# Grouped steps at the two ends of a stretch: block maxima from the copies, sums by a product with ones, separate PSUM banks for pairs and single items

## The chip, the cores and the metric

The kernel runs on one core of one Trainium2 chip. The metric is the device time of one execution in microseconds (us); the median of 3 runs of the kernel before is 3428.8 us (3427.73 to 3429.0). Engines are named as in the profile: PE multiplies matrices (its weight loads, PEld, run beside it), DVE is the vector engine, ACT the scalar engine, POOL the GpSimd engine, SP issues DMAs.

## The reference

Four cross-attention layers follow each other on x, of shape (4 batches, 512 positions, 256 channels), with a context of shape (4, 1024, 512), all in float32. Layers 0, 2 and 3 have 16 heads of 64, two columns of keys that a mask suppresses, a bias and a residual ("masked" layers). Layer 1 has an RMS norm ahead, 16 query heads of 16, and 4 heads of keys and values that four query heads share each ("grouped" layer).

```python
# layers 0, 2, 3
q, k, v = hidden @ Wq, context @ Wk, context @ Wv          # 16 heads of 64
logits = einsum('bhqd,bhkd->bhqk', q, k) * 64 ** -0.5 + col_bias
out = softmax(logits) @ v                                   # per head
x = out @ Wo + bo + hidden
# layer 1
xn = rmsnorm(x) * norm_w                                    # 16 heads of 16, 4 heads of k and v
x = x + (softmax(xn @ wq @ (context @ wk).T / 4) @ (context @ wv)) @ wo
```

## The kernel before, in words

**Units and steps.** A layer of a batch is cut into 8 units. A masked unit is two heads (64 rows each), a grouped unit two heads (of 16 rows, padded to 32). A unit's softmax stands with its 1024 keys in 8 blocks of 128 partitions and its two heads' 512 queries side by side, so one block is 128x1024 and fills two of the eight PSUM banks. The program has 96 steps (two strings, `MASKED_TURNS` and `GROUPED_TURNS`, say which unit comes when); each step has one masked unit `g`, and 32 of them, in four stretches of 8, have a grouped unit `lam` beside it. The batches are interleaved, so the grouped layer of one batch runs beside a masked layer of another. PE is given its instructions in the order of the program, and each engine works through its own in order.

**What a step does.** In order: `scores(g)` (L859): 8 blocks of logits, two matmuls each (L869; the first block also takes the mask by two small products, L875), each block copied by ACT from PSUM into the store `st` (L879). `attend(g1)` (L902): the products of the exponentials of the step before with the values, 16 matmuls of 64 columns. Then a list `fill` of PE work: output projections (L1108), the next queries (L766), keys (L552) or values (L605) of later units (in steps without grouped units by L665, with seven products for eight), among them `attend(lam)`. If the next step has a grouped unit, `coming`, its logits are made in this step as four **pairs** of blocks (`logits_pair`, L842 and the copy L848), which a list `pairs` sets between the entries of `fill` by a clock that adds up written estimates, 12.0 + 2.5 i.

**Maximum and exponentials.** The largest logit of each query is taken off. DVE spreads the maximum over all partitions (`max_quarters` L946 to L953, `max_everywhere` L966), then subtracts: DVE for masked units (L974), POOL for grouped ones (L972). ACT takes the exponentials (L980). POOL adds up the 8 blocks of a masked unit (`running_sum`, L1019); the sum over the partitions of that, and its reciprocal, come one step later. A grouped unit gets its sums from a column of ones in the values.

**Two ways, by a flag.** `tabled[0]` says for each step which way it goes; it is set where the step has a grouped unit and the next one has one too (`lam and coming`), 28 of the 96 steps.

- Flag off: block 0 stays in its two banks, DVE maximises the other 7 copies into it (L886 for scores, L857 for pairs: read PSUM and `st`, write PSUM) and reduces it (L926). Sums: `normalise` (L1066) late in the step: DVE alone, 10 instructions (L926, L1051 to L1062) and the scaling L1088. PSUM banks are taken from all eight, the longest free first.
- Flag on: each block's banks are given back after the copy, DVE reduces each copy to a column of a small table (`block_max`, L926 `tops<-st`) and the table at the end (L942). Sums: `sums_beside` (L1070), in the same step's `fill`: PE multiplies the running sum by ones (L1074, two matmuls of 64 columns, 4 records in the trace), DVE transposes, inverts and transposes back (L805 to L807), then L1088. Pairs of banks are taken from 0 to 3 (0 to 5 for scores), single banks from 4 to 7 (class `Place`, L103).

So a stretch of 8 grouped units has 7 steps of the second way, and at its ends two steps of the first: an **opening** step, with `coming` but no `lam` (they start at 378.22, 798.60, 1218.27 and 2426.59 us), and a **closing** step, with `lam` but no `coming` (719.63, 1139.30, 1558.77 and 2767.64 us). In an opening step the coming unit is the first of its batch; its queries (L781) and values (L743) are made at the head of `fill`. A bank is free for PE once its last reader is through: in these steps that is the copy of a block, the last subtraction (the two banks of the spread maximum, `mb_place`), the residual addition L1136 or L1140 (those of an output projection), the scaling L1088 (the bank `po` of `attend`) or `max_quarters`.

Of the kernel before, what the change touches and what calls it, by code (L numbers as in the profile page):

```python
# [20 lines left out]
NT = T // P  # L21
# [59 lines left out]
def kernel(ctx: ExitStack, tc: tile.TileContext, a: dict, out: bass.AP):  # L81
# [9 lines left out]
    def t_(shape, tag, name, bufs=1, dtype=FP):  # L91
        return sb.tile(shape, dtype, tag=tag, name=name, bufs=bufs)
# [8 lines left out]
    tabled = [False]  # L101
# [27 lines left out]
    def st_slot(n):  # L129
        return st_all[:, n // (NT + 1), n % (NT + 1), :]  # L130
# [6 lines left out]
    def give_set(g):  # L137
        sets_free.append(g.set)
# [660 lines left out]
    def reciprocal_rows(out_, in_, room):  # L799


        turned = room[:, 0:S]
        short = t_([P, S // 32, 1], "short", f"short{len(turns)}")
        turns.append(0)
        nc.vector.transpose(turned, in_)  # L805
        nc.vector.reciprocal(short, turned.rearrange("p (c r) -> p c r", r=32)[:, :, 0:1])
        nc.vector.transpose(  # L807
            out_.rearrange("p (c r) -> p c r", r=32), short.to_broadcast([P, S // 32, 32])
        )
# [3 lines left out]
    def norm_square(b):  # L813
        gq[b, "xn"] = t_([P, KC, S], "xn", f"xn{b}")
        nc.scalar.activation(gq[b, "xn"], xs[1, b], AF.Square)

    def rms_norm(b, room):
        x, xn, nw = xs[1, b], gq[b, "xn"], columns["L1_xattn_norm_w"]
        w = Place(1)
        m = w.ap  # L820
        for k in range(KC):
            nc.tensor.matmul(m, lhsT=ones, rhs=xn[:, k, :], start=(k == 0), stop=(k == KC - 1))

        def evacuate():
            inv = t_([P, S], "stage", f"inv{b}")
            nc.scalar.activation(inv, m, AF.Sqrt, bias=eps, scale=1.0 / C)
            w.back()
            reciprocal_rows(inv, inv, room)
            for k in range(KC):
                nc.vector.scalar_tensor_tensor(  # L830
                    xn[:, k, :], x[:, k, :], nw[:, k : k + 1], inv, ALU.mult, ALU.mult
                )

        return evacuate
# [53 lines left out]
    def place_out(g, width=1):  # L888
        g.place = Place(width)
        g.po, g.psum = g.place.ap[:, 0:S], g.place.ap[:, S:]  # L890

    def attend(g, blocks=range(NT)):
        for t in blocks:
            for j in range(2):
                rows = g.rows[j]
                if not g.masked:
                    rows = slice(64 * g.h + 32 * j, 64 * g.h + 32 * (j + 1))
                at, first, last = rows, 0, NT - 1
                if not g.masked:
                    at = slice(64 * (t % 2) + 32 * j, 64 * (t % 2) + 32 * (j + 1))  # L900
                    first, last = t % 2, NT - 2 + t % 2
                nc.tensor.matmul(  # L902
                    g.po[at, :], lhsT=g.v[:, t, rows], rhs=g.st[t][:, j * S : (j + 1) * S],
                    start=(t == first), stop=(t == last),
                )

    def keep_even(g):


        if g.h == 0:  # L910
            gq[g.b, "o"] = t_([P, S], "o1", f"o1_{g.name}")
        nc.scalar.copy(gq[g.b, "o"][64 * g.h : 64 * (g.h + 1), :], g.po[0:64, :])

    def keep_odd(g):
        half = gq[g.b, "o"][64 * g.h : 64 * (g.h + 1), :]
        nc.vector.tensor_tensor(half, half, g.po[64:128, :], ALU.add)
        if g.h == 0:
            g.place.back()
# [102 lines left out]
    def turn_grouped(g):  # L1021
        normalise_grouped(g, g.place.ap)
        g.place.back()
# [46 lines left out]
    def sums_beside(g):  # L1070
        w = Place(1, among=range(8))
        m = w.ap
        for j in range(2):
            nc.tensor.matmul(  # L1074
                m[g.rows[j], :], lhsT=ones[:, 0:64], rhs=g.acc[:, j * S : (j + 1) * S],
                start=True, stop=True,
            )

        def turned():
            g.ot = t_([P, S], "ot", f"ot_{g.name}", bufs=3)  # L1080
            reciprocal_rows(g.ot, m, g.ot)
            w.back()
            scale_out(g)

        return turned

    def scale_out(g):
        nc.vector.tensor_tensor(g.ot, g.po, g.ot, ALU.mult)  # L1088
        g.place.back()
# [99 lines left out]
    def at(n):  # L1189
        return steps[n] if 0 <= n < len(steps) else (None, None)  # L1190
# [8 lines left out]
    def head(g):  # L1199
        return steps[step_of[1, g.b, 0]][1]  # L1200
# [26 lines left out]
    g0, g1 = masked[0:2]  # L1227
# [24 lines left out]
    def keys(*of):  # L1252
        return [
            (1.7 if each.masked else 3.4, lambda h=h, part=part, each=each: k_part(each, h, part))
            for h in range(2 if of[0].masked else 1) for each in of for part in range(2)
        ]
# [27 lines left out]
    for n in range(len(steps) + 2):  # L1284
        g, lam = at(n)
        follows, coming = at(n + 1)
        tabled[0] = bool(lam and coming)
        soon = at(n + 2)[1]
        g1, attended = attended, g
        ending = n >= len(steps) - 2  # L1290
# [60 lines left out]
        late = []  # L1351
        pairs = []
# [5 lines left out]
        def behind_exponentials():  # L1358
            pass_events(99.0)
            while late:  # L1360
                late.pop(0)()
# [17 lines left out]
        by_ones = tabled[0]  # L1379
# [32 lines left out]
                    events.append((2.0 * t - 7.5, lam, lambda t=t: exponentials(lam, t)))  # L1412
            events.sort(key=lambda e: e[0])
        if coming:
            pairs += [(12.0 + 2.5 * i, i) for i in range(NT // 2)]

# [2 lines left out]
        def behind(add):  # L1421
            if g is not masked[-1]:
                return add
            late.append(add)

        fill, of_grouped = (
            [
                (1.8 * len(each), lambda each=each: behind(project_out(*each)))
                for each in outs if each[0].masked == m
            ]  # L1430
            for m in (True, False)
        )
# [4 lines left out]
        if fast_k:  # L1437
# [3 lines left out]
            fill = of_keys[:2] + fill + of_keys[2:4] + of_queries + of_keys[4:]  # L1441
        elif fast_v:
            of_values = fast_values(g)
            if fresh:
                of_values[1:4] = of_values[3:4] + of_values[1:3]
                fill = of_values[:2] + fill + of_grouped + of_values[2:4] + of_queries + of_values[4:]
                of_grouped = []
            else:
                fill = of_values[:2] + fill + of_queries + of_values[2:]
# [7 lines left out]
        if lam:  # L1457

            def attend_grouped():
                while any(of is lam for _, of, _ in events):  # L1460
                    events.pop(0)[2]()
                lam.v = head(lam).v
                place_out(lam)
                attend(lam)
                give_set(lam)
                late.append(lambda: keep_odd(lam))
                if lam.h == 1:
                    late.append(lambda: turn_grouped(lam))
                return lambda: keep_even(lam)

            total, where = 0.0, 0
            while where < len(fill) and total < (8.0 if by_ones and of_values else 9.5):
                total += fill[where][0]
                where += 1
            fill.insert(where, (3.6, attend_grouped))
            if by_ones:
                fill.insert(where, (1.0, lambda: late.insert(0, sums_beside(g1))))
        if soon and soon.first:

            def square():  # L1480
                behind_exponentials()
                norm_square(soon.b)

            of_keys = keys(soon)
            fill += of_keys[:1] + [(0.0, square)] + of_keys[1:]
            room = st_slot((NT + 1) * ctx_whole[soon.b][0] + NT)
            fill.append((1.7, lambda: rms_norm(soon.b, room)))
# [19 lines left out]
        for us, w in fill:  # L1507
            while pairs and pairs[0][0] <= now:
                pair(pairs.pop(0)[1])
                now += 1.0  # L1510
                pairs = [(max(at, now + 1.6), i) for at, i in pairs]
# [42 lines left out]
```

## Time and profile before

| | us |
|---|---|
| median of 3 runs | 3428.8 (3427.73 to 3429.0) |
| the profiled execution's own time | 3429.2 |
| its span, first to last instruction | 3427.4 (granted clock 0.999) |
| the four opening steps | 45.46, 45.17, 45.17, 45.41 |
| the four closing steps | 38.64, 38.64, 38.64, 38.65 |
| steps with the flag on, keys in `fill` (L552) | 43.46 to 45.48 |
| busy: PE, DVE, POOL, ACT | 3402.1, 2971.5, 2592.5, 2346.9 |

A step is measured from the start of its first L869 to that of the next step's. A line of the timeline gives the start, the time from the first to the end of the last of a row of equal instructions, the engine, line and shape, how many, and in brackets the idle time of the engine ahead of them with what ended it. Ends of matmuls are modelled, so the time that a row of matmuls takes is read here from its start to the start of the next row.

### The profile page before, as it was taken

To read this page: it belongs to the slowest core of one execution; us is meant where nothing else is said; L and a number is where in the kernel's file an instruction comes from. 1 tells how busy PE (TensorE), PEld (TensorE's weight loads), DVE (VectorE), ACT (ScalarE), POOL (GpSimd) and SP (SyncE) were. 2 spreads that over 40 slices of the span, in tenths; PEclk is the share of its full clock that TensorE was granted. 3 is DMA by queue.
4 is the path that set the end of the run, shared out by engine and by line. 5 is a ranking of instruction groups with operands and counts; after the bars stand their busy time and mean duration, and the time that the engine had idled before them with its cause. 6 is when DMAs were issued, how large, how long until landed. Compare 5 with 4: busy or idle time off the path is not lost.

```text
span 3427.4 us, 42731 instructions
## 1 busy us (share of the span) xinstructions
PE 3402.1 (99%) x15488; PEld 1652.1 (48%) x15488; DVE 2971.5 (87%) x3915; ACT 2346.9 (68%) x2729; POOL 2592.5 (76%) x1337
## 2 busy tenths in 40 slices
PE   9999999999999999999999999999999999999999
PEld 5555444444444444444455554554444445454554
DVE  7888889988889889998888888888888988889887
ACT  5666688776777767776656666666677866666665
POOL 4888488875888668888678768677588888769675
PEclk9999999999999999999999999999999999999999
DMA  3232111011100121011001111011101101011100
GB/s 105 67 114 86 57 36 51 30 48 37 54 27 30 48 62 30 27 30 45 28 28 53 34 36 43 28 53 56 37 30 51 36 21 53 28 40 56 35 30 10
DMA packets 147734, 151.70 MB, mean 44 GB/s; under 512 B 23608, under 2 KB 125496, under 8 KB 147012
## 3 DMA queue, kind: packets, MB, share of 16 engines
q1 hardware_dynamic: 144958, 140.58, 13.2%
q0 software_dynamic: 2560, 8.39, 0.9%
q8 instruction: 123, 2.02, 0.2%
q14 instruction: 87, 0.71, 0.1%
q10 hardware_dynamic: 6, 0.00, 0.0%
HBM read 132.15 MB, written 15.73 MB: 43 GB/s over the span
## 4 chain that ended last, share of the span: by engine, by line
PE 91%; DVE 7%; ACT 1%; issue 1%; DMA 0%; DVEq 0%; POOL 0%; ACTq 0%
PE ps L902 21%; PE ps L665 19%; PE ps L869 18%; PE ps L605 8%; PE ps L552 8%; PE ps L842 5%; PE ps L766 5%; PE ps L1108 5%; DVE ps L886 2%; DVE st L974 2%; PE ps L1074 1%; PE ps L567 1%; PE ps L875 1%; DVE ps L926 0%; PE ps L416 0%
## 5 line engine op out<-in xcount | busy, mean ns | idle before, releaser
L1019 POOL TENSOR_TENSOR st<-st 128x1024 f32<-128x1024 f32 x668 | 1581.5, 2367 | 566.3 <-ACT st L980 521.5
L980 ACT ACTIVATE st<-st 128x1024 f32<-128x1024 f32 x1024 | 1038.3, 1059 | 225.0 <-POOL st L972 109.7
L974 DVE TENSOR_TENSOR st<-st,ps 128x1024 f32<-128x1024 f32 x768 | 883.9, 1213 | 3.3
L902 PE MATMUL ps<-st,v 128*64 128x512 f32 (+1 forms) x4064 | 789.8, 595 | 0.0
L886 DVE TENSOR_TENSOR ps<-ps,st 128x1024 f32<-128x1024 f32 x476 | 586.7, 1233 | 210.9 <-ACT st L879 167.8
L972 POOL TENSOR_TENSOR st<-st 128x1024 f32<-128x1024 f32 x256 | 598.0, 2378 | 225.8 <-DVE st L966 185.4
L879 ACT COPY st<-ps 128x1024 f32<-128x1024 f32 x768 | 713.6, 1049 | 63.7 <-PE ps L875 58.2
L869 PE MATMUL ps<-qt,kt 64*128 64x512 f32 x3008 | 689.2, 596 | 4.0 <-DVE every L953 4.0
L926 DVE TRANSPOSE_TENSOR_REDUCE tops<-st 128x32 f32<-128x1024 f32 x448 | 517.6, 1212 | 43.6 <-ACT st L848 41.9
L902 PEld LDWEIGHTS ps<-st,v 128*64 128x64 f32 (+1 forms) x4064 | 239.9, 130 | 534.9 <-issue 447.5
L869 PEld LDWEIGHTS ps<-qt,kt 64*128 64x128 f32 x3008 | 280.9, 186 | 351.0 <-ACT st L879 143.8
L605 PE MATMUL ps<-wv,ctx 128*128 128x256 f32 x1344 | 313.7, 386 | 1.1 <-issue 1.1
L665 PE MATMUL ps<-st 128*128 128x128 f32 (+1 forms) x1620 | 308.6, 339 | 3.3 <-ACT ps L688 3.3
L552 PE MATMUL ps<-ctx,wk 128*128 128x512 f32 x672 | 310.4, 603 | 0.2 <-ACT ctx L428 0.2
L848 ACT COPY st<-ps 128x1024 f32<-128x1024 f32 x256 | 246.9, 1017 | 86.5 <-PE ps L842 85.8
L605 PEld LDWEIGHTS ps<-wv,ctx 128*128 128x128 f32 x1344 | 250.9, 191 | 93.1 <-issue 56.3
L665 PEld LDWEIGHTS ps<-st 128*128 128x128 f32 x1620 | 214.3, 192 | 95.5 <-issue 86.9
L680 ACT COPY st<-ps 128x512 f32<-128x512 f32 x45 | 26.4, 586 | 339.3 <-PE ps L665 339.3
L552 PEld LDWEIGHTS ps<-ctx,wk 128*128 128x128 f32 x672 | 122.0, 189 | 179.7 <-issue 163.4
L766 PE MATMUL ps<-x,wq 128*128 128x512 f32 x376 | 180.4, 602 | 1.1 <-ACT x L391 1.1
L842 PE MATMUL ps<-qt,kt 32*128 32x512 f32 x1024 | 171.5, 640 | 6.3 <-DVE ot L1088 5.2
L1108 PE MATMUL ps<-ot,wo 128*128 128x512 f32 x380 | 173.2, 598 | 0.0
(201 smaller groups left out, 3001.8 us busy)
## 6 DMA issues: line engine op xcount, KB each, us to landing
wv<-in_L_xattn_Wv_dram SPq DMA_DIRECT2D x48, 512.0 KB
ctx<-kept SPq DMA_DIRECT2D x24, 1024.0 KB
wk<-in_L_xattn_Wk_dram SPq DMA_DIRECT2D x47, 512.0 KB
wo<-in_L_xattn_Wo_dram SPq DMA_DIRECT2D x96, 128.0 KB
wq<-in_L_xattn_Wq_dram SPq DMA_DIRECT2D x94, 128.0 KB
st<-kept SPq DMA_DIRECT2D x4, 2048.0 KB
qt<-q SPq DMA_DIRECT2D x64, 128.0 KB
kept<-st SPq DMA_DIRECT2D x12, 512.0 KB
```

The costliest lines, as they stand in the source:

```text
L552: nc.tensor.matmul(m, lhsT=g.w["k"][:, k, :], rhs=ctx_half[g.b, n][:, k, :], start=(k == 0), stop=(k == KT - 1),)
L605: nc.tensor.matmul(m[:, half * 2 * P : (half + 1) * 2 * P], lhsT=ctx_half[g.b, t // 4][:, k, t % 4 * P : (t % 4 + 1) * P], rhs=g.w["v2"][: ...
L665: nc.tensor.matmul(m if is_keys else m[:, q], lhsT=right[:, k, :] if is_keys else left_[:, k, q], rhs=left_[:, k, :] if is_keys else right ...
L869: nc.tensor.matmul(m[:, j * S : (j + 1) * S], lhsT=g.kt[g.rows[j], keys], rhs=g.qt[g.rows[j], :], start=True, stop=t > 0,)
L879: nc.scalar.copy(g.st[t], m)
L886: nc.vector.tensor_tensor(top, top, g.st[t], ALU.max)
L902: nc.tensor.matmul(g.po[at, :], lhsT=g.v[:, t, rows], rhs=g.st[t][:, j * S : (j + 1) * S], start=(t == first), stop=(t == last),)
L926: nc.vector.tensor_reduce(out_, of.rearrange("p (b x) -> p b x", x=32), AX.X, op, apply_transpose=True)
L972: nc.gpsimd.tensor_tensor(g.st[t], g.st[t], g.mb, ALU.subtract)
L974: nc.vector.tensor_tensor(g.st[t], g.st[t], g.mb, ALU.subtract)
L980: nc.scalar.activation(st, st, AF.Exp)
L1019: nc.gpsimd.tensor_tensor(g.acc, g.st[0] if t == 1 else g.acc, g.st[t], ALU.add)
```

## The change

The flag is set for `lam or coming`, so the opening and closing steps go the second way as well: 36 steps in place of 28. The matmuls of `sums_beside` get a place in the `fill` of an opening step, and the clock of its pairs starts 1.0 later, which is what that entry adds to it. In a closing step the existing lines insert them ahead of `attend(lam)`. The choice of banks in `Place` and the branches in `scores`, `logits_pair` and `max_quarters` follow the flag and are not edited.

```diff
-        tabled[0] = bool(lam and coming)
+        tabled[0] = bool(lam or coming)
...
-            pairs += [(12.0 + 2.5 * i, i) for i in range(NT // 2)]
+            pairs += [((13.0 if coming.first else 12.0) + 2.5 * i, i) for i in range(NT // 2)]
...
             if by_ones:
                 fill.insert(where, (1.0, lambda: late.insert(0, sums_beside(g1))))
+        elif by_ones:
+            fill.insert(2, (1.0, lambda: late.insert(0, sums_beside(g1))))
```

In its order of instructions the changed program has on PE 16 matmuls L1074 more, two in each of the eight steps, and no other change of order; in an opening step they stand between L766 and the first L552, in a closing step between the third L552 group and the grouped L902. ACT and POOL have the same instructions in the same order. On DVE an opening step loses 7 L886, 7 L857, 2 L926 that read PSUM and the 10 instructions of L926 and L1051 to L1062, and gets 16 L926 that read the copies, 2 L942 and L805 to L807; a closing step the same without L857's half.

## The prediction

> **What bounds the kernel now.** First the page's busy times, then the waits of PE, then the timeline of PE in an opening and a closing step, last the same rows in a step that has the flag on already.
>
> ```profile
> PE 3402.1 (99%) x15488; PEld 1652.1 (48%) x15488; DVE 2971.5 (87%) x3915; ACT 2346.9 (68%) x2729; POOL 2592.5 (76%) x1337
> ```
>
> ```profile
> PE ps L842 <- DVE ot L1088: 5.2, 4, 1.3
> PE ps L869 <- DVE every L953: 4.0, 4, 1.2
> ```
>
> PE is busy 99% of the span, and its idle time is some 25 us. Two rows of waits are the largest, and each occurs four times: once in each opening step (a pair waits for L1088) and once in each closing step (a block of scores waits for L953).
>
> [...] Equal matmuls start at a fixed distance: 12 L552 of 128x512 take 5.24 us to the next row, 0.43 us each, in every step, and L902 x32 takes 7.02 us in all. A row that takes longer than its sisters has a wait in it. By that measure PE streams nearly everywhere, and what is to be gained is found row by row.
>
> An opening step, around its pairs:
>
> ```profile
> 820.94 1.88 PE L766 MATMUL ps<-x,wq 128*128 128x512 f32 x4
> 822.65 3.60 PE L552 MATMUL ps<-ctx,wk 128*128 128x512 f32 x8
> 826.18 1.78 PE L842 MATMUL ps<-qt,kt 32*128 32x512 f32 x8
> 827.89 1.98 PE L552 MATMUL ps<-ctx,wk 128*128 128x512 f32 x4
> 831.17 1.14 PE L842 MATMUL ps<-qt,kt 32*128 32x512 f32 x8 [1.29 <-DVE ot L1088]
> ```
>
> A closing step, at its scores:
>
> ```profile
> 1140.47 1.02 PE L869 MATMUL ps<-qt,kt 64*128 64x512 f32 x4
> 1142.72 5.42 PE L869 MATMUL ps<-qt,kt 64*128 64x512 f32 x24 [1.23 <-DVE every L953]
> 1148.08 7.09 PE L902 MATMUL ps<-st,v 128*64 128x512 f32 x32
> ```
>
> And a step with the flag on, with the product and the pairs as the changed steps will have them:
>
> ```profile
> 655.10 5.31 PE L552 MATMUL ps<-ctx,wk 128*128 128x512 f32 x12
> 660.34 1.08 PE L1074 MATMUL ps<-st,ones 128*64 128x512 f32 x4
> 661.35 3.64 PE L902 MATMUL ps<-st,v 128*32 128x512 f32 x32
> 664.92 1.14 PE L842 MATMUL ps<-qt,kt 32*128 32x512 f32 x8
> 665.99 1.98 PE L552 MATMUL ps<-ctx,wk 128*128 128x512 f32 x4
> 667.90 1.35 PE L842 MATMUL ps<-qt,kt 32*128 32x512 f32 x8
> 669.19 1.98 PE L552 MATMUL ps<-ctx,wk 128*128 128x512 f32 x4
> ```
>
> Here the scores after the mask (L869 x28) take 6.10 us from start to start, a pair 1.07 or 1.28, and the product 1.01.
>
> **The change, part by part.** PE keeps all its work and order, so a changed step is its old length, plus the product, minus the waits that go.
>
> *Product with ones.* Its 4 records stream in 4 x 0.214 = 0.86 us (L902 x32 streams in 6.86); in steps that have it, it takes 1.01 up to the next row. In closing steps it stands ahead of L902 as there: +1.01. In opening steps it stands between two rows of 128 columns. There I add 0.10, by which L766 x4 takes longer ahead of a row of another shape (1.82 for 1.72): +1.11. Sum 4 x 1.01 + 4 x 1.11 = **+8.5 us**. Bounds: 0.86 and 1.11 each, 6.9 to 8.9. It needs the running sum (POOL's L1019), which in both kinds of step ended before the step began (in the closing one at 1137.5, 1.8 ahead), and a bank. The bank of the opening step was last read by ACT's L785, over at 20.7 us of the step, and PE gets there at 23.9; in the closing step by L1140, over at 20.0 to 22.0 in steps with the flag on, and PE gets there at 24.8. So I let it wait for nothing. Behind it on PE stands the whole rest of the step.
>
> [...]
>
> *Closing step.* The wait is for a single bank in which the maximum of the grouped unit was made at the end of the step before; the flag-off step takes its pairs of banks from all eight and runs into it. With the flag on, scores stay in banks 0 to 5 and that bank lies in 4 to 7; steps with the flag on have the same predecessor and take 6.10 to 6.11 for L869 x28, against 7.59, 7.60, 7.60 and 7.61 in the closing steps. So 1.48 to 1.50 goes, 1.01 comes: **-0.48 a step, -1.9 us**. What could be late next is `attend(lam)`: POOL's subtractions start on L966 as before (4.86 us into the step) and end at 23.5, PE starts L902 at 25.8 and reaches its eighth block 3 us later. DVE's subtractions start 0.8 earlier, at 17.1 (17.4 in the flag-on step at 463.77, whose maximum of the grouped unit ends 0.3 later). The next step starts with 6.10 now and finds its banks as before.
>
> *Opening step.* Waits in the four: the first pair takes 2.23, 1.71, 1.94 and 2.17 for 1.07 (its second two banks are `mb_place`, free after the last L974, which ends 28.5, 28.2, 28.2 and 28.4 us into the step); the L552 x4 behind it 3.28 for 1.91 (the next pair waits for L1088, as block 0's banks are held and one bank of the only other free two is `po`). With the flag on the pairs use banks 0 to 3 and wait only for copies. DVE: 8 L926 start 1.14 apart where 7 L886 start 1.34 apart, and L942 (0.66 to the next) replaces L926 (1.30), so the last L974 ends 0.75 earlier, at 27.4 to 27.7. PE reaches the first pair at 27.35 + 1.11 = 28.46 (28.69 in the second of the four, whose scores take 6.33): no wait. From there I take the rows of the flag-on step: 1.07 + 1.91 + 1.28 + 1.91 + 1.07 + 1.91 + 1.28, and 5.35 for the last L552 x12 as now, 15.78 in all. The steps end at 44.24 (second: 44.47): savings of 1.22, 0.70, 0.93 and 1.17, **-4.0 us**, product included. The copies keep up: ACT's L848 starts 1.2 us after its pair, at 29.7, after the last exponential (28.5) and L557. Bound: in the step at 463.77 ACT was late, and the same rows took 2.37 and 1.97 where I use 1.91 and 1.28. That would cost 1.15 a step, 4.6 us.
>
> *DVE's own savings* (some 3.6 us in an opening step: 14 L886 and L857 and the short sums go, 16 L926 come; about 3 in a closing one) lie beside PE and count only through the waits above. The maximum of the coming unit ends about 1 us after the end of an opening step, now 2.3 to 2.5; POOL starts the next step's subtractions that much earlier, and PE does not wait there (40.09 us, the shortest of their kind, in all four). ACT, POOL and SP get nothing more. The other 88 steps keep order and banks, relabelled.
>
> Sum: -1.9 - 4.0 = -5.9, on the profiled execution's 3429.2: **3423.3 us**. That execution lies 0.4 above the median of the runs; I predict 3423.2.
>
> **Rivals.**
>
> *ACT late at the pairs.* The copies take the place of L1088 as what the second pair waits for. For it: 8 of the 28 flag-on steps show most of it. Against it: there ACT is behind with grouped exponentials, and an opening step has none. 3423.2 + 4.6 = 3427.8.
>
> *PE has more slack than its rows show:* the product is swallowed. The waits that go are 5.9 in the closing and 8.5 in the opening steps, 14.4 together, so 3429.2 - 14.4 = 3414.8. For it: a row's end is modelled. Against it: start-to-start distances are as exact where the product already stands. [...]
>
> *The waits move on: slower.* In closing steps the third block, in opening steps the second pair, would wait as long for a copy by ACT (L879, L848) as now for DVE, since fewer banks are open to them (six, and four). Price: the product with nothing returned, +8.5, 3437.7. It decides as soon as less than 8.5 of the 14.4 comes back. Against it: ACT sits idle for 7.4 us ahead of L785 in an opening step, and the flag-on steps have no such wait in their scores.
>
> **How the numbers follow.** What can be told from no change is about 0.2%, 6.9 us, so the line lies at 3422.3, one microsecond under my forecast. Forecast 77%, of which about a third falls under the line when the product costs 0.86 to 1.0 a step or the last pairs wait less; its own range is 3421 to 3425.5. ACT late 10%, slack 8%, waits move on 5%. Faster 0.25 + 0.08 = 0.33, slower 0.05, within 0.2% the remaining 0.62. The range runs from the product at its lower bound in all eight steps (8.5 - 6.9 = 1.6 less: 3421.6, and 1.3 for the spread of the runs, rounded) to ACT late in all four: 3420.0 to 3428.0.
>
> **What would show it.** Right: L1074 144 times; no PE wait for L953 or L1088; L869 x28 at 6.1 in closing steps, which last 38.15; opening steps of 44.2 to 44.5, pairs at 1.07 and 1.28. Wrong: an idle time ahead of L1074 or right behind it; L842 rows of 1.9 with a wait for L848; any of the 88 other steps with another length, above all those after the eight.

## The result, and the profile after

The changed kernel takes **3423.06 us** (median of 20 runs, 3421.99 to 3424.98) where the kernel before, run beside it, takes 3428.95 (20 runs, 3427.54 to 3429.36): a ratio of 0.9983, 95% interval 0.9977 to 0.9990. That is 5.9 us less. Its profiled execution took 3422.26, its span is 3420.5. The busy times of the page:

```profile
PE 3405.4 (100%) x15520; PEld 1652.9 (48%) x15520; DVE 2957.1 (86%) x3871; ACT 2347.0 (69%) x2729; POOL 2594.1 (76%) x1337
```

PE has 32 records more and 3.3 us more of busy time, yet the span is shorter: what went is idle time. The waits of PE (engine, line, releaser; us in all, times, longest):

```profile
PE ps L665 <- ACT ps L688: 3.3, 4, 1.3
...
PE ps L766 <- DVE x L1140: 0.2, 1, 0.2
```

The two rows that led this list, L842 for L1088 and L869 for L953, are gone. The last row is the only new wait (the 1.1 us ahead of L605, at the start of the program, stood in the list before under another releaser). The timeline of PE in the opening step that was shown before (it starts at 795.30 us now):

```profile
817.41 1.88 PE L766 MATMUL ps<-x,wq 128*128 128x512 f32 x4
819.22 1.08 PE L1074 MATMUL ps<-st,ones 128*64 128x512 f32 x4
820.23 3.70 PE L552 MATMUL ps<-ctx,wk 128*128 128x512 f32 x8
823.86 1.14 PE L842 MATMUL ps<-qt,kt 32*128 32x512 f32 x8
824.93 1.98 PE L552 MATMUL ps<-ctx,wk 128*128 128x512 f32 x4
```

Read from start to start: L766 takes 1.81 (1.71 before), the product 1.01, the 8 L552 3.63 (3.53 before), the first pair 1.07 and the L552 behind it 1.91 (1.71 and 3.28 before). And the closing step that starts at 1135.01:

```profile
1136.18 6.17 PE L869 MATMUL ps<-qt,kt 64*128 64x512 f32 x28
1142.29 7.09 PE L902 MATMUL ps<-st,v 128*64 128x512 f32 x32
...
1159.80 1.08 PE L1074 MATMUL ps<-st,ones 128*64 128x512 f32 x4
1160.81 3.64 PE L902 MATMUL ps<-st,v 128*32 128x512 f32 x32
```

The scores are one unbroken row of 6.11, and the product takes 1.01.

| step lengths, us | before | after |
|---|---|---|
| opening steps | 45.46, 45.17, 45.17, 45.41 | 44.38, 44.36, 44.36, 44.38 |
| closing steps, each | 38.64 | 38.16 |
| the eight together | | 5.67 less |
| start of the first scores (L869) | 33.40 | 31.94 |
| other steps that differ by over 0.1 | | -0.29, -0.27, +0.35, +0.22 |

The first two of these other steps are inner steps (28 steps have the flag on in both kernels; these two start at 461.24 and 964.70 us). In each a row at the pairs is shorter: an L552 takes 2.08 for 2.37 in the one, the last pair 1.28 for 1.56 in the other. The first saving recurs in all versions below that have both the block maxima and the product in the opening steps, the second in all versions with block maxima in the closing steps, so both most likely come with the change; how is not shown. The two longer steps have no grouped unit, and in most other versions such a difference stands at other steps or nowhere.

The start of the program, 1.46 us shorter here, has nothing to do with the change: it is a stretch at half the granted clock that one execution has and another has not (8 L605 take 3.68 us in it and 1.99 without it, the last section). It is why the two profiled executions lie 6.9 apart and the medians 5.9.

### The profile page after: what moved, and what is told of

Same layout as the page of the kernel before. It is cut to its first block, busy times and chain, and to the rows that moved or that the text cites. A ratio compares the mean times of both kernels' runs of the same rounds, so it can differ in the third digit from the quotient of the medians.

```text
span 3420.5 us, 42705 instructions
## 1 busy us (share of the span) xinstructions
PE 3405.4 (100%) x15520; PEld 1652.9 (48%) x15520; DVE 2957.1 (86%) x3871; ACT 2347.0 (69%) x2729; POOL 2594.1 (76%) x1337
## 4 chain that ended last, share of the span: by engine, by line
PE 94%; DVE 3%; ACT 1%; issue 1%; POOL 0%; DMA 0%; DVEq 0%; ACTq 0%
PE ps L902 22%; PE ps L665 19%; PE ps L869 19%; PE ps L605 8%; PE ps L552 8%; PE ps L1108 5%; PE ps L766 5%; PE ps L842 5%; DVE ps L886 2%; PE ps L1074 1%; DVE st L974 1%; PE ps L567 1%; PE ps L875 1%; PE ps L781 0%; PE ps L416 0%
## 5 line engine op out<-in xcount | busy, mean ns | idle before, releaser
L974 DVE TENSOR_TENSOR st<-st,ps 128x1024 f32<-128x1024 f32 x768 | 884.3, 1215 | 3.3
L902 PE MATMUL ps<-st,v 128*64 128x512 f32 (+1 forms) x4064 | 789.8, 595 | 0.0
L886 DVE TENSOR_TENSOR ps<-ps,st 128x1024 f32<-128x1024 f32 x420 | 517.8, 1233 | 206.8 <-ACT st L879 169.1
L869 PE MATMUL ps<-qt,kt 64*128 64x512 f32 x3008 | 687.0, 596 | 0.0
L926 DVE TRANSPOSE_TENSOR_REDUCE tops<-st 128x32 f32<-128x1024 f32 x544 | 628.4, 1212 | 59.3 <-ACT st L848 53.8
L902 PEld LDWEIGHTS ps<-st,v 128*64 128x64 f32 (+1 forms) x4064 | 239.8, 130 | 535.2 <-issue 451.3
L869 PEld LDWEIGHTS ps<-qt,kt 64*128 64x128 f32 x3008 | 280.9, 186 | 344.9 <-ACT st L879 146.0
L605 PE MATMUL ps<-wv,ctx 128*128 128x256 f32 x1344 | 312.0, 384 | 1.1 <-ACT ctx L428 1.1
L552 PE MATMUL ps<-ctx,wk 128*128 128x512 f32 x672 | 310.7, 603 | 0.0
L848 ACT COPY st<-ps 128x1024 f32<-128x1024 f32 x256 | 246.8, 1017 | 83.2 <-PE ps L842 83.0
L605 PEld LDWEIGHTS ps<-wv,ctx 128*128 128x128 f32 x1344 | 249.9, 190 | 92.7 <-issue 55.1
L552 PEld LDWEIGHTS ps<-ctx,wk 128*128 128x128 f32 x672 | 121.6, 189 | 180.5 <-issue 164.6
L766 PE MATMUL ps<-x,wq 128*128 128x512 f32 x376 | 180.4, 602 | 1.3 <-ACT x L391 1.1
L842 PE MATMUL ps<-qt,kt 32*128 32x512 f32 x1024 | 168.5, 640 | 0.8
```

The lines of the kernel that those rows point to most:

```text
L552: nc.tensor.matmul(m, lhsT=g.w["k"][:, k, :], rhs=ctx_half[g.b, n][:, k, :], start=(k == 0), stop=(k == KT - 1),)
L605: nc.tensor.matmul(m[:, half * 2 * P : (half + 1) * 2 * P], lhsT=ctx_half[g.b, t // 4][:, k, t % 4 * P : (t % 4 + 1) * P], rhs=g.w["v2"][: ...
L869: nc.tensor.matmul(m[:, j * S : (j + 1) * S], lhsT=g.kt[g.rows[j], keys], rhs=g.qt[g.rows[j], :], start=True, stop=t > 0,)
L886: nc.vector.tensor_tensor(top, top, g.st[t], ALU.max)
L902: nc.tensor.matmul(g.po[at, :], lhsT=g.v[:, t, rows], rhs=g.st[t][:, j * S : (j + 1) * S], start=(t == first), stop=(t == last),)
L926: nc.vector.tensor_reduce(out_, of.rearrange("p (b x) -> p b x", x=32), AX.X, op, apply_transpose=True)
```

## The experiments

Each is the changed kernel with one edit, unless it says otherwise. Times are medians. Each ratio is to runs of the kernel before of the same series: 3427.64 us (29 runs) for the product alone, the banks from all eight, the first version with DVE's sums and the first without any product; 3427.51 (21 runs) for the opening steps alone, the banks in closing steps only and the next two with DVE's sums; 3428.9 (7 runs) for the last two.

**Opening steps alone.** Do the two halves of the change depend on each other?

```diff
-        tabled[0] = bool(lam or coming)
+        tabled[0] = bool(coming)
```

> The change in the opening steps alone; closing steps as before. If the two ends are independent: opening steps 44.4 us (0.8 to 1.1 less than before), closing 38.64, in all 3425.2 against 3428.95 before; if the closing steps' gain hangs on the opening ones, 3423 or 3429.

Measured: 3423.9 us (11 runs), ratio 0.9989 (0.9980 to 0.9998), 3.6 less. Opening steps 44.38, 44.36, 44.36, 44.38, as in the changed kernel; closing steps 38.64 and the wait for L953 back at 4.0 us, four times. The ends are independent, and the opening steps bring two thirds.

**The product alone, in all 36 steps.** Maxima and banks of the eight steps go back to the first way.

```diff
-        tabled[0] = bool(lam or coming)
+        tabled[0] = bool(lam and coming)
...
-        by_ones = tabled[0]
+        by_ones = bool(lam or coming)
```

> Only the sums by a product with ones in the eight steps; maxima into the held block and any bank, as before the change. Theory A (the opening step's waits are for the end of DVE's subtractions and of L1088; the product alone holds PE back by 1.2 us at the first pair and lets L1088 end 1.9 us earlier, so both waits go): opening steps 44.4 us as in the changed kernel; closing steps keep the wait for L953 and pay 1.01, 39.65; in all 3429.2. Rival B (the held block and the mixed banks cause the opening's waits): opening steps stay above 45.5, closing 39.65, in all 3434.

Measured: 3428.54 us (11 runs), ratio 1.0002 (0.9993 to 1.0011). Closing steps 39.64: the product's 1.00 on top of 38.64. But opening steps 44.50, 44.36, 44.36, 44.45, within 0.12 of the changed kernel. Its pairs in the timeline of PE:

```profile
826.95 1.14 PE L842 MATMUL ps<-qt,kt 32*128 32x512 f32 x8
828.02 1.98 PE L552 MATMUL ps<-ctx,wk 128*128 128x512 f32 x4
```

1.07 and 1.91, no wait, with the maximum made in block 0's banks and all eight banks open. So neither the block maxima nor the separate banks are needed to clear the opening step: the product does it alone. It does so in two ways. In the step at 378.05 PE comes to the first pair 28.56 us into the step (27.35 before), just after the last L974 ends (28.46). And DVE's L1088 ends at 30.85 (32.81 before), ahead of the second pair at 31.55.

**Banks from all eight.** Maxima and product stay; the choice of banks in `Place` goes by a flag of its own.

```diff
+        apart[0] = bool(lam and coming)
...
-                if tabled[0]:
+                if apart[0]:
```

> The changed kernel, but in the eight steps any bank may go to a pair or a single item (longest free first); maxima from the copies and the product stay. Theory A (the closing step's wait is for the one bank in which the grouped maximum was made, which the third block then takes): closing steps 39.4 to 39.7 us with a PE wait for L953 of 1.2, opening steps 44.3 to 44.4, in all 3428.5. Rival B (giving a block's banks back after its copy is what removes it): closing steps 38.16, in all 3423.

Measured: 3425.82 us (11 runs), ratio 0.9995 (0.9986 to 1.0004). Closing steps 39.65, since the wait is back:

```profile
1136.51 1.02 PE L870 MATMUL ps<-qt,kt 64*128 64x512 f32 x4
1138.76 5.42 PE L870 MATMUL ps<-qt,kt 64*128 64x512 f32 x24 [1.22 <-DVE every L954]
```

(Lines are one higher in this kernel.) Opening steps are 43.93, 0.42 to 0.45 *shorter* than with separate banks: all four pairs take 1.07, where with banks 0 to 3 every second one takes 1.28 to 1.31. That had not been expected, and leads to the next.

**Separate banks in closing steps only** (the flag above, set otherwise):

```diff
-        apart[0] = bool(lam and coming)
+        apart[0] = bool(lam)
```

> The changed kernel, only that in opening steps pairs and single items may use any bank (closing and inner steps keep them apart). Theory A (separate banks pay in closing steps alone, and cost 0.44 us in opening steps, as the steps of the run with any bank showed): opening steps 43.93, closing 38.16, in all 3421.3. Rival B (the 0.44 came from the order of banks that the closing steps left behind): opening steps 44.4, 3423.

Measured: 3421.13 us (11 runs), ratio 0.9980 (0.9971 to 0.9989). Opening 43.93, closing 38.16. Separate banks pay in the closing steps, 1.49 each, and cost in the opening ones, 0.44 each.

**Sums by DVE in the eight steps.** Maxima and banks stay, the product goes there.

```diff
-        by_ones = tabled[0]
+        by_ones = bool(lam and coming)
...
-            pairs += [((13.0 if coming.first else 12.0) + 2.5 * i, i) for i in range(NT // 2)]
+            pairs += [(12.0 + 2.5 * i, i) for i in range(NT // 2)]
```

> The changed kernel, but in the eight steps at the ends of the stretches DVE makes the sums (the old chain L926, L1051 to L1062), not PE: maxima from the copies and separate banks stay. Theory A (the product costs PE its own time, 1.20 us in an opening and 1.01 in a closing step, and nothing waits for the longer DVE chain, since the pairs take banks 0 to 3 and the scaled output lies in 4 to 7): opening steps 43.2 us, closing 37.15, 8.8 us under the changed kernel, 3414.2. Rival B (the short sums are what lets DVE keep up: with 4.35 us of DVE work in place of 2.4 the coming unit's maximum comes late and the next step's scores or subtractions wait): opening steps 44 and over, 3419 to 3424.

Measured: 3425.57 us (11 runs), ratio 0.9995 (0.9986 to 1.0004): the number of neither theory. Opening 43.70, 43.42, 43.43, 43.66 and closing 37.15. The closing steps are shorter by the product, as theory A has it, the opening ones by 0.68 to 0.95. But the four steps *behind* the closing ones are 2.3, 4.0, 1.55 and 2.82 longer. The waits of PE name the releaser:

```profile
PE ps L869 <- DVE o L1035: 7.3, 4, 2.0
```

And DVE, in the closing step at 1135.05, shows why L1035 is late:

```profile
1156.71 5.73 DVE L974 TENSOR_TENSOR st<-st,ps 128x1024 f32<-128x1024 f32 x5
1169.56 1.26 DVE L926 TRANSPOSE_TENSOR_REDUCE ps<-st 128x32 f32<-128x1024 f32 x1 [7.12 <-ACT kt L557]
```

DVE is not overloaded, it stands idle for 7.12 us ahead of the sums. These need a scratch bank (`reciprocal_sums`, L1046). With the flag on only 4 to 7 are open to it, and the one it gets is read last by ACT's copy L557 of a group of keys, late in the step. Of the 10.7 us that the four steps lose, two stretches of 3.41 us at half the granted clock, behind the wait, make some 3.4 (an estimate, half of each; last section).

**The same, with the scratch bank from all eight:**

```diff
-        w = Place(1)
+        w = Place(1, among=range(8))
```

> As the run with sums by DVE in the eight steps, but the scratch bank of those sums may be any free one, where there it had to lie in 4 to 7 and waited in the closing steps for the copy of the fifth group of keys (DVE idle from 27.6 to 34.5 us of the step, and the next step's scores late by 1.5 to 4 us). Theory A (that bank was the whole loss, not DVE's load): closing steps 37.15 and the steps behind them 40.33 and 31.62 again, opening steps 43.4 to 43.7, in all 3415.8. Rival B (DVE's longer chain is late even so): the steps behind the closing ones stay longer, 3419 to 3425.

Measured: 3415.93 us (5 runs), ratio 0.9964 (0.9951 to 0.9978). The same place on DVE:

```profile
1159.92 1.21 DVE L974 TENSOR_TENSOR st<-st,ps 128x1024 f32<-128x1024 f32 x1
1161.05 1.25 DVE L926 TRANSPOSE_TENSOR_REDUCE ps<-st 128x32 f32<-128x1024 f32 x1
```

No idle time; closing steps 37.15, the steps behind them 40.33 and 31.62 as in the changed kernel. Opening steps stay at 43.70, 43.41, 43.42, 43.66, so the waits for L1088 are gone without the product too. The first two pairs still take 1.14 to 1.43 and 1.48, so less than the product's own time comes back. Either is enough for the waits on L1088: the product alone, or the maxima and banks alone.

**And any bank in the opening steps** (the edits of the last two together with the flag of `Place`):

```diff
+        apart[0] = bool(lam)
```

> The same, and in opening steps pairs and single items may use any bank; closing and inner steps keep them apart. Theory A (with four banks every second pair waits some 0.2 us for a copy; with more it does not, and the sums' scratch is free at 30.0 us when the second pair comes at 30.3): opening steps 42.7 to 43.0, in all 3412.6 to 3414. Rival B (pairs then wait for the sums' scratch bank or the next step's second block waits for the maximum of the coming unit): opening steps 43.5 or more or the steps behind them longer, 3416 and over.

Measured: 3412.19 us (5 runs), ratio 0.9955 (0.9941 to 0.9968). Opening 43.08, 42.80, 42.80, 43.05, closing 37.15: 2.4 and 1.5 under the kernel before, 15.5 in the eight. The first pair of an opening step and the row behind it:

```profile
820.51 1.21 PE L843 MATMUL ps<-qt,kt 32*128 32x512 f32 x8
821.66 1.98 PE L553 MATMUL ps<-ctx,wk 128*128 128x512 f32 x4
```

The second pair takes 1.07. With neither the product nor separate banks in these steps, the block maxima by themselves clear the waits for L1088.

**Sums by DVE in all 36 steps**, no product anywhere (its place in `fill` stays, with nothing in it):

```diff
-            if not ending and not by_ones:
+            if not ending:
...
-                fill.insert(where, (1.0, lambda: late.insert(0, sums_beside(g1))))
+                fill.insert(where, (1.0, lambda: None))
```

> The changed kernel with the sums by DVE in all 36 steps with the flag on, no product with ones anywhere. Theory A (a product costs PE 1.0 us, but in the 28 inner steps DVE is busy nearly throughout, so its extra 1.9 us make the grouped maximum, POOL's subtractions and the exponentials late and the pairs wait): some of the 28 us comes back, 3392 to 3410, with the waits in the steps with keys. Rival B (only PE counts): 3423 - 8.8 - 28 x 1.01 = 3386. Rival C (DVE becomes the bound and falls behind from step to step): 3425 and over.

Measured: 3439.09 us (6 runs), ratio 1.0035 (1.0023 to 1.0047). Pairs wait for ACT's copies (L842 for L848) 22.4 us in 19 places, and some steps with the flag on grow by 2 to 4. I took it that DVE's ten instructions make the exponentials, and so the copies, late. But two things are mixed here, since the scratch bank was restricted in these steps too. DVE in the step at 881.52:

```profile
909.60 1.26 DVE L926 TRANSPOSE_TENSOR_REDUCE ps<-st 128x32 f32<-128x1024 f32 x1 [0.69 <-ACT kt L557]
```

**So once more, with the scratch bank from all eight:**

```diff
-        w = Place(1)
+        w = Place(1, among=range(8))
```

> Sums by DVE in all 36 steps (no product anywhere), the scratch bank of the reciprocal sums taken from all eight. The run without the product and with the scratch bank restricted gave 3439.1 us, and two things were mixed in it: steps 20, 30, 40 and 76 were 2.3, 2.3, 1.5 and 1.5 us longer through the scratch bank (7.7 in all), the 28 inner steps 17.5 us longer in sum. Theory A: the inner loss is ACT, which comes late to the copies of the pairs since DVE's ten instructions of the sums delay the subtractions and so the exponentials; the bank has no part in it. Then the four steps are back at 40.33 and 31.6, the waits of pairs for L848 stay near 22 us, and the time is 3439.1 - 7.7 = 3431.4. Theory B: the inner loss comes through the scratch bank as well; then the waits for L848 fall to a few us, the inner steps are 0.9 shorter than with the product, and the time is below 3400.

Measured: 3411.73 us (4 runs), ratio 0.9949 (0.9932 to 0.9965). Theory A falls: the 28 inner steps, 17.3 us longer in sum than in the changed kernel with the restricted bank, are 2.9 shorter without the restriction, so the whole loss came through the bank. There a wait of 0.7 us on DVE had made the maximum of the coming unit 0.7 later, and the next step 4.0 longer (44.68 for 40.65). Most of these 4.0 us are the clock. In the windows of that step, with the restricted bank (length; busy time and instructions of PE, PEld, DVE, ACT, POOL; granted clock; DMA):

```profile
957.10:959.90 2.80, 2.77 (x8) 0.73 (x8) 2.79 (x3) 1.90 (x2) 2.72 (x2) 0.69 0.00 0
959.90:963.60 3.70, 3.70 (x10) 2.52 (x8) 2.00 (x2) 1.01 (x1) 3.54 (x3) 0.50 0.00 0
963.60:966.00 2.40, 2.40 (x12) 1.10 (x12) 0.00 (x0) 1.04 (x2) 1.81 (x1) 0.71 0.00 0
```

The missing shares of the clock, 0.31, 0.50 and 0.29, make 3.4 us (an estimate: each share times the length of its window). The clock records of this execution have nine stretches of 3.41 us at half the clock in seven of the inner steps, which by the same count make 15.4 of the 17.3 us. So the bank made the waits, and by this estimate what the waits cost was mostly the half clock behind them.

Theory B's number is not reached either, as taking the product out gives back little in the inner steps. PE's waits at the pairs in this kernel, and then PE in an inner step of the changed kernel (546.52) and in the same step here (548.49):

```profile
PE ps L842 <- DVE short L1056: 4.6, 8, 0.8
...
PE ps L842 <- ACT st L848: 3.3, 10, 0.5
```

```profile
571.31 1.08 PE L1074 MATMUL ps<-st,ones 128*64 128x512 f32 x4
...
576.97 1.98 PE L552 MATMUL ps<-ctx,wk 128*128 128x512 f32 x4
579.05 2.04 PE L842 MATMUL ps<-qt,kt 32*128 32x512 f32 x8
581.03 1.98 PE L552 MATMUL ps<-ctx,wk 128*128 128x512 f32 x4
```

```profile
576.86 1.13 PE L842 MATMUL ps<-qt,kt 32*128 32x512 f32 x4
578.49 1.13 PE L842 MATMUL ps<-qt,kt 32*128 32x512 f32 x4 [0.51 <-DVE short L1056]
...
581.46 1.60 PE L842 MATMUL ps<-qt,kt 32*128 32x512 f32 x8
583.00 1.98 PE L552 MATMUL ps<-ctx,wk 128*128 128x512 f32 x4
```

PE comes to its pairs 1.01 earlier and waits there as much longer. The changed kernel has a wait there too: its L552 and its second pair take 2.08 and 1.98, where such rows take 1.91 and 1.07 to 1.28 elsewhere. The L552 behind the second pair starts at 34.51 us of the step in both, and both steps last 44.32. ACT's first copy of the pairs (L848) starts at 31.47 us of the step in both, right behind its exponentials, so ACT sets the pace there. Of the inner steps nine are shorter than in the changed kernel, four by 0.86 to 0.88 and five by 0.28; the rest lie between 0.1 below and 0.3 above it, but one, at 461.79, is 1.5 longer. There the clock was at half for one stretch, which by the same estimate costs 1.7:

```profile
493.25:496.66 3.41, 3.41 (x4) 0.97 (x4) 3.24 (x6) 2.18 (x3) 3.33 (x2) 0.50 0.00 0
```

In most of the inner steps nothing is gained when DVE's sums take the product's place. What the product costs there with nothing in its place was not run.

**The two best together:** sums by DVE in all 36 steps, scratch bank from all eight, any bank in the opening steps:

```diff
-            if not ending and not by_ones:
+            if not ending:
...
-        w = Place(1)
+        w = Place(1, among=range(8))
...
+        apart[0] = bool(lam)
```

> The version with sums by DVE in the eight end steps, free scratch bank, and any bank in the opening steps (3412.2 us), with the product taken out of the 28 inner steps as well. Theory A (DVE's sums make ACT late at the pairs of the inner steps): the inner steps are 17.5 us longer in sum, 3429.7 us, and pairs wait for L848 some 22 us. Theory B (it was the scratch bank): each inner step is 0.9 shorter, 3387 us.

Measured: **3409.45 us** (4 runs), ratio 0.9943 (0.9926 to 0.9960), 19.5 under the kernel before and the lowest of all versions here. Neither theory's number, for the reasons just given. It lies 2.3 below the version before it, since the opening steps are 0.6 shorter each; the intervals of the two overlap, so their order rests on these step lengths.

## Why the prediction was right, point by point

- **The sum** was -5.9, on two kinds of steps; the eight steps gave -5.67 and the medians -5.9. That the medians agree to a tenth is luck: between runs that start alike (last section) the two kernels lie 5.5 to 5.6 apart. The two kinds of wait went as forecast, and none of the three rivals came true in these eight steps. Of the other 88, which were to stay as they are, four differ by 0.22 to 0.35, with a sum of 0.0; two of them probably come with the change.
- **Product, closing: +1.01.** Measured 1.01 by its row, and 1.00 by the version with the product alone.
- **Product, opening: +1.11. This term was mis-sized:** 1.21. I counted the 0.10 by which the row ahead takes longer (L766, 1.71 to 1.81) and not the 0.10 of the row behind (L552 x8, 3.53 to 3.63). The product stands between two rows of another shape, which makes two changes of shape, and the prediction prices one. Its own lines had both prices: L552 x4 between two pairs takes 1.91, where 4 x 0.43 is 1.72, so 0.10 on each side. (That 12 L552 take 5.24 in every step is not so either: its sum uses 5.35 for those behind a pair.) In this trace each of these two changes of shape cost 0.10 us. The product costs 4 x 1.01 + 4 x 1.21 = 8.9 in place of 8.5: the sum's upper bound, and above the bound of 1.11 for an opening step.
- **Closing: -0.48 a step.** Measured -0.48 to -0.49. The cause, separate banks, is shown by the version without them: 39.65, the wait back at 1.22.
- **Opening: -1.22, -0.70, -0.93, -1.17.** Measured -1.08, -0.82, -0.81, -1.03. The 0.10 that was not priced is in each. The second went the other way since I had let its scores stay at 6.33: they take 6.11 now, so a wait of 0.22 that I had counted as lasting went too.
- **Why the opening waits go: half right.** The prediction put it down to the pairs' banks, DVE's faster maxima and PE coming later, together. The runs show that the product is enough by itself (44.36 to 44.50), through the later PE at the first pair and the earlier L1088 at the second, and that without it the maxima are enough (43.41 to 43.70 with separate banks, 42.80 to 43.08 with any). So the size would have come out without the pairs' banks; the prediction joined causes of which fewer suffice. What the banks add in the opening step is a loss, 0.44, in the very 1.28 rows that the prediction took from the steps with the flag on.
- **DVE's savings beside PE:** right but for some 0.6 us. DVE's busy time fell by 14.4 us, and beyond the eight steps only the two inner steps that are 0.29 and 0.27 shorter may show it.
- **ACT late at the pairs:** not in these eight steps. In inner steps, once no scratch bank is late, what the pairs wait for in the version without any product is in part such a copy (3.3 us in ten places).
- **Product swallowed:** wrong for the eight steps, where taking it out gives 1.0 in closing and 0.7 to 0.95 in opening steps. For most of the steps that had it already, giving the sums to DVE gains nothing. PE is busy 100% of the span by the page of the changed kernel's profile, and yet where the product of 1.01 us went from the step at 546.52 and DVE made the sums, the step lasted 44.32, as with it.
- **Waits move on:** not seen in this change. A wait that moved through a bank did come in the versions with DVE's sums, at a place the prediction had not looked at: the scratch bank of the sums.

So the change takes out 14.6 us of waits (8.9 + 5.67) and pays 8.9 of it for a product that the eight steps do not need: with DVE's sums there, a free scratch bank and any bank in the opening steps, the eight steps are 15.5 shorter than before.

## What to carry to other kernels

When a change bundles several parts, each wait that it removes should be tried against each part alone: here the product and the block maxima each removed one wait, and a third part (the banks) gained at one end of the stretch and lost at the other. When a step grows behind an engine that seems overloaded, look for an idle time on that engine first: twice (7.12 and 0.69 us of it on DVE) it was not load but one PSUM bank, chosen by its time of return and not by the engine that reads it last. An inserted product cost its row, 1.01 us, where PE set the pace, and 0.10 us more for each change of shape that it brought; where the copies of another engine set the pace, giving its sums to DVE gained nothing in most steps (44.32 us with the product and without in one of them). And a step that grows by more than its wait, as the one that grew by 4.0 us behind a wait of 2.03 did, should be read with the granted clock beside it (0.51 there).

## What the runs showed of the hardware

Runs of one kernel fall on two levels some 1.4 us apart: 3427.5 to 3427.8 and 3428.7 to 3429.4 for most of the kernel before's, 3422.0 to 3422.3 and 3423.0 to 3423.9 for most of the changed one's. In the profiled executions the difference is in one place. In the windows of 18.0 to 21.5 us (busy time and instructions by engine, then the granted clock), first the kernel before, then the changed one:

```profile
18.00:21.50 3.50, 3.42 (x8) 2.66 (x9) 3.33 (x7) 0.02 (x1) 2.66 (x3) 0.53 0.80 222
```

```profile
18.00:21.50 3.50, 2.98 (x17) 2.48 (x17) 3.33 (x7) 0.54 (x2) 2.70 (x3) 1.00 0.81 228
```

The clock is at half for one stretch, 3.413 us from 18.21 by the clock records, and 8 L605 take 3.68 us where they take 1.99 in the other. PE waits of 1.1 us stand ahead of it, in both executions. Of the twelve profiled executions six have this stretch, with the first scores at 33.17 to 33.45 us, and six do not, with 31.77 to 32.86. Within a level the two kernels lie 5.5 to 5.6 us apart. In the version with DVE's sums and the restricted bank, the same came in mid-kernel, behind a wait of 2.03 us:

```profile
1177.29:1180.70 3.41, 3.41 (x8) 1.47 (x10) 2.59 (x3) 1.01 (x1) 0.00 (x0) 0.51 0.26 65
```

That step (at 1172.19) grew by 4.0, its sister at 753.75 by 2.3, with the clock at 1.00 throughout: the half clock cost 1.7 more in one of two like places. (The two others behind closing steps grew by 1.55 and 2.82; the second has such a stretch from 2805.54.) In the inner step at 461.79 of the version without any product, the wait of PE ahead of the half clock is listed as 0.79 us (1.90 by its rows). What decides which wait brings it, and whether a run has it, is not settled here.
